# Masked attention with four engines in balance: ten double-mask steps at new places, and a transposition queued behind its own step's mask

## The chip, the core and the metric

The kernel runs on one core of a Trainium2 chip. The core has five engines that follow queues of their own and wait for each other by semaphores: TensorE (PE, matrix products; its weight loads are shown apart as PEld), VectorE (DVE), ScalarE (ACT), GpSimd (POOL), and SyncE (SP), which here only issues DMAs. The metric is the device time of one execution in microseconds (us); lower is better.

## What is computed

Three graph attention layers with eight heads of 16, each followed by a feed-forward part, and then a last layer of a different kind, on 16 sequences of 1024 tokens with 128 features. One adjacency matrix of 1024 x 1024 serves all sequences. Cut to what matters here:

```python
Q, K, V = ((h @ W).reshape(B, N, 8, 16) for W in (Wq, Wk, Wv))
scores = einsum('bnhd,bmhd->bhnm', Q, K) / sqrt(16)
scores = where(adj == 0, -inf, scores)
x = h + (einsum('bhnm,bmhd->bnhd', softmax(scores), V).reshape(B, N, 128) @ Wo + bo)
x = layer_norm(x)
x = layer_norm(x + relu(x @ W1 + b1) @ W2 + b2)      # three times; then
e = leaky_relu(s_i[:, :, None] + s_j[:, None, :])    # last layer, one head
out = layer_norm(softmax(where(adj == 0, -inf, e)) @ (x @ W) + x)
```

## The kernel before

**Tiling.** A block is one sequence in one of the three layers: 48 blocks, numbered 0 to 47, in groups of four sequences (all four in layer 0, then in layer 1, then in layer 2). A block has 32 steps. A step is a choice of head half `g` (four heads), query half `qh` (512 queries) and key tile `kt` (128 keys); eight steps with the same `g` and `qh` make a half, which adds up in one PSUM accumulator, `acc`. Below, "step 11" is the twelfth step of a block.

**One step** (`score_step`, L532). The four heads are two pairs. For each pair TensorE writes the scores of 128 keys by 2 x 512 queries into a PSUM tile `s` (L540); there are three such tiles, and the pool gives a new pair one that is free. The scores become masked exponentials in the SBUF tile `e` in one of two ways:

- by POOL: ScalarE takes the exponential out of PSUM (L548), and POOL multiplies it by a 0/1 mask in SBUF (L549). Only the first pair of a step can go this way.
- by VectorE: VectorE adds a large negative mask while it reads PSUM (L552), and ScalarE takes the exponential in SBUF (L564). The second pair always goes this way; the first goes this way too in the steps of a block that the table `BOTH_ON_DVE` (L41) lists.

Four steps later (`AHEAD`, L40) TensorE multiplies the exponentials by the values into `acc` (`av_step`, L566, matmul L569). So the last value matmul of a half comes in step 11, 19, 27 or, of the last half, in step 3 of the next block. After it `finish` (L572) transposes `acc` on VectorE (L580) into `tt`, takes the reciprocal of the row sums (L583), and POOL multiplies them into `A` (L584). There is one `acc`, so the value matmuls of the next half wait for this transposition.

**Other work.** Between the steps the kernel weaves in tasks, by tables of steps (`AT`, L34): the projections of the next block, in which ScalarE takes the upper part `hi` of a projection (L467, L471) and VectorE the remainder `lo` (L468, L472) at steps 9, 11, 17 and 19; the output projection and the two feed-forward matmuls of the block before (L378), with VectorE's transposes of `A` (L598, two of them in step 9, followed by two small range reductions, L448), additions and statistics (L415, L408, L410) and POOL's normalisation (L428 to L436, four or eight slices) and scaling (L627, L506, L510); transposes of `x` by VectorE (L352) and DMA; and, in twelve blocks at the turn of the groups, the tasks of the last layer (`last_tasks`), with masks of their own on VectorE (L776).

**What sets the order.** The order of TensorE, ScalarE and SyncE is the order of the program text (`tc.manual_schedule`). On VectorE and POOL a scheduler chooses by priorities: `soon()` raises the priority of what stands under it, and `tc.issue_after(x)` makes an instruction stand behind `x` in its queue. Two dictionaries hold such anchors: `low[n]` is the remainder taken in step `n`, and `behind["dve"]` is VectorE's latest mask, which in `finish` is the last mask of the step just issued, since `score_step` of a step is called before its `av_step`. A mask in L551 stands behind the remainder of two steps before, where there was one. `finish` in L579 follows the same rule for the transposition: that of step 11 stands behind the remainder of step 9, that of step 19 behind that of step 17, and the other two are free. [...]

Of the kernel before, what the change touches and what calls it, by code (L numbers as in the profile page):

```python
# [37 lines left out]
STACK_AT = 24  # L38
AT_END = {3: (12, 21, 22, 24, 25, 26, 27, 28, 30, 31), 2: (8, 9, 13, 14, 15, 16, 17, 18, 20, 21)}
AHEAD = 4  # L40
BOTH_ON_DVE = (2, 6, 7, 8, 17, 21, 23, 25, 26, 29, 30)  # L41
TILES = {"w": 8, "x": LANES + 1, "last": 2}
BLOCKED = -57344.0

# [75 lines left out]
def fast_path(ctx: ExitStack, tc: tile.TileContext, a: dict, out: bass.AP, flag):  # L120
# [24 lines left out]
    head, tail = [True], [False]  # L145
# [182 lines left out]
    def soon():  # L328

        return nullcontext() if head[0] else tc.high_priority(offset=SOON)  # L330
# [185 lines left out]
    behind, low = {}, {}  # L516
# [15 lines left out]
    def score_step(step):  # L532
# [3 lines left out]
        for pp in range(2):  # L536
# [6 lines left out]
            psv = ps.rearrange("p (r q) -> p r q", q=512)  # L543
            both = now[0] % (4 * NT) in BOTH_ON_DVE
            on_pool = pp == 0 and not both
# [26 lines left out]
    def finish(g, qh, acc):  # L572

        def run():
            if g == 0 and qh == 0:
                state["A"] = work.tile([P, 2, 16, G, HD], F32, tag="A", name="A", bufs=1)
                state["recs"] = work.tile([P, G, 2, 16], F32, tag="recs", name="recs", bufs=2)
            tt = work.tile([P, 16, SLOT], F32, tag="tt", name="tt", bufs=1)
            with soon(), tc.issue_after(low[now[0] - 2]) if now[0] - 2 in low else nullcontext():  # L579
                nc.vector.transpose(tt.rearrange("p a b -> p (a b)"), acc)  # L580
            rec = state["recs"][:, g, qh, :]
            with soon():
                nc.vector.reciprocal(rec, tt[:, :, HD])  # L583
                nc.gpsimd.tensor_mul(state["A"][:, qh, :, g, :], tt[:, :, :HD],  # L584
                                     rec[:, :, None].to_broadcast([P, 16, HD]))
        return run
# [243 lines left out]
    now = [0]  # L830
# [404 lines left out]
```

## Time and profile before

| what | before |
|---|---|
| time, median of 3 runs | 3988.66 us (3985.82 to 3991.97) |
| time of the profiled execution | 3988.0 us |
| its span, first to last instruction | 3985.9 us |
| mean granted TensorE clock | 0.975 |

The numbers of the profile are from that one execution. "Busy" is the time in which an engine executes something; instructions that follow each other overlap a little, so that a mean duration is longer than the distance between two starts. In the table of groups each row is a line of the kernel on one engine: what it writes and reads with the sizes, how often, then total busy time in us and mean in ns, then the idle time of the engine just ahead of these instructions and who ended it. Two more of its rows belong to the change:

```profile
L569 PE MATMUL acc<-e,v 128*17 128x512 f32 x12288 | 1641.5, 606 | 52.2 <-POOL e L549 48.1
L580 DVE STREAM_TRANSPOSE tt<-acc 128x512 f32<-128x512 f32 x192 | 135.6, 706 | 36.2 <-PE acc L569 36.2
```

The first is the value matmul, the second the transposition of a finished half: its 36.2 us of idle time are spent waiting for the last value matmul of that half.

### The profile page before, as it was taken

What the parts mean: (1) busy time and instruction counts of PE and PEld (TensorE: products, weight loads), DVE (VectorE), ACT (ScalarE), POOL (GpSimd) and SP (SyncE); (2) the same over time, 40 slices, a digit from 0 to 9 for tenths busy, and PEclk for the clock granted to TensorE, in tenths of its full rate; (3) what the DMA queues carried; (4) which work ended last, traced back from release to release, by engine and by line L of the source; (5) the groups of instructions that cost most, each with busy time, mean ns of one, the idle gap of its engine ahead of it and who ended that gap; (6) DMA issues with size and microseconds to landing.
All of it is one profiled execution on the core that took longest, in us unless ns stands there. A gap on an engine that the chain in (4) does not pass through costs nothing.

```text
span 3985.9 us, 108397 instructions
## 1 busy us (share of the span) xinstructions
PE 3735.5 (94%) x43873; PEld 1501.6 (38%) x43873; DVE 3480.8 (87%) x5844; ACT 3289.4 (83%) x3797; POOL 3393.9 (85%) x2923
## 2 busy tenths in 40 slices
PE   7999999999999999998999999999999999999887
PEld 2333333344433333334444333333444433333346
DVE  6889999988889999998888999998888899999765
ACT  7989999977778999996776999998767799999750
POOL 4889999977789999997778999998778899999784
PEclk8999999999999999999999999999999999999998
DMA  5423424322223424332222423333222333324100
GB/s 139 114 65 92 100 71 111 80 66 65 66 66 87 111 69 104 84 90 67 62 67 68 112 67 102 88 85 98 66 55 66 86 75 99 94 73 115 49 7 20
DMA packets 245880, 319.19 MB, mean 80 GB/s; under 512 B 51072, under 2 KB 174208, under 8 KB 245376
## 3 DMA queue, kind: packets, MB, share of 16 engines
q1 hardware_dynamic: 243840, 311.52, 31.3%
q8 instruction: 349, 5.72, 0.6%
q14 instruction: 155, 1.27, 0.1%
q10 hardware_dynamic: 1536, 0.68, 0.1%
HBM read 58.53 MB, written 51.38 MB: 28 GB/s over the span
## 4 chain that ended last, share of the span: by engine, by line
PE 44%; DVE 23%; ACT 10%; POOL 8%; issue 6%; SPq 2%; DMA 1%; ACTq 0%; DVEq 0%; POOLq 0%
PE acc L569 16%; DVE e L552 16%; PE t L378 14%; PE s L540 11%; ACT e L564 5%; ACT e L548 3%; POOL e L549 2%; ACT hT L644 2%; POOL x L436 2%; PE s L378 1%; POOL x L440 1%; DVE st L408 1%; POOL x L441 1%; POOL mv L430 1%; DVE aT L598 1%
## 5 line engine op out<-in xcount | busy, mean ns | idle before, releaser
L552 DVE TENSOR_TENSOR e<-s,mask_add 128x1024 f32<-128x1024 f32 x2064 | 2410.6, 1209 | 166.7 <-PE s L540 133.6
L549 POOL TENSOR_TENSOR e<-e,mask 128x1024 f32<-128x1024 f32 x1008 | 2030.6, 2029 | 436.3 <-ACT e L548 435.5
L564 ACT ACTIVATE e<-e 128x1024 f32<-128x1024 f32 x2064 | 2145.0, 1061 | 190.6 <-DVE e L552 171.6
L569 PE MATMUL acc<-e,v 128*17 128x512 f32 x12288 | 1641.5, 606 | 52.2 <-POOL e L549 48.1
L540 PE MATMUL s<-Wq,Wk 64*128 64x512 f32 x6144 | 1237.7, 464 | 84.6 <-ACT e L548 29.8
L548 ACT ACTIVATE e<-s 128x1024 f32<-128x1024 f32 x1008 | 1032.2, 1024 | 311.7 <-PE s L540 311.0
L540 PEld LDWEIGHTS s<-Wq,Wk 64*128 64x128 f32 x6144 | 509.0, 186 | 1218.4 <-DVE e L552 492.6
L569 PEld LDWEIGHTS acc<-e,v 128*17 128x17 f32 x12288 | 205.6, 95 | 552.3 <-issue 418.4
L436 POOL TENSOR_SCALAR x<-x,mv 128x128 f32<-128x128 f32 x896 | 391.3, 453 | 19.2
L430 POOL TENSOR_TENSOR mv<-mv,half_neg 128x4 f32<-128x4 f32 (+1 forms) x179 | 214.3, 1197 | 14.7
L415 DVE TENSOR_TENSOR x<-t,x 128x512 f32<-128x512 f32 x191 | 132.0, 691 | 106.0 <-PE t L378 102.4
L378 PE MATMUL t<-x1T,W 128*32 128x512 f32 x1520 | 200.8, 600 | 5.1 <-DVE parts L743 3.2
L408 DVE BATCH_NORM_STATS2 st<-x 128x6 f32<-128x128 f32 x896 | 198.1, 281 | 6.3
L378 PEld LDWEIGHTS t<-W,hT 128*32 128x32 f32 x6080 | 173.8, 112 | 63.9 <-issue 57.0
L378 PE MATMUL t<-hd,e 128*32 128x129 f32 x6656 | 194.9, 274 | 3.0 <-DVE lo L468 3.0
L776 DVE SCALAR_TENSOR_TENSOR e<-s,mask 128x256 f32<-128x256 f32 x512 | 175.1, 411 | 22.0 <-PE s L772 21.9
L378 PE MATMUL t<-W,hT 128*32 128x128 f32 x6080 | 187.7, 276 | 2.9 <-DVE parts L743 2.9
L378 PEld LDWEIGHTS t<-hd,e 128*32 128x32 f32 x6656 | 182.1, 109 | 17.3 <-DVE lo L468 6.3
L580 DVE STREAM_TRANSPOSE tt<-acc 128x512 f32<-128x512 f32 x192 | 135.6, 706 | 36.2 <-PE acc L569 36.2
L644 ACT ACTIVATE hT<-t,b 128x512 f32<-128x512 f32 x190 | 131.0, 690 | 22.5 <-PE t L378 21.8
L510 POOL TENSOR_TENSOR x<-x,bo 128x1024 f32<-128x1024 f32 x48 | 114.9, 2393 | 9.7 <-PE s L378 7.2
L584 POOL TENSOR_TENSOR A<-tt,recs 128x256 f32<-128x256 f32 x192 | 120.3, 627 | 3.0 <-DVE recs L583 3.0
(141 smaller groups left out, 2450.1 us busy)
## 6 DMA issues: line engine op xcount, KB each, us to landing
Wk<-hi SPq DMA_DIRECT2D x384, 128.0 KB
Wk<-lo SPq DMA_DIRECT2D x384, 128.0 KB
Wq<-hi SPq DMA_DIRECT2D x384, 128.0 KB
Wq<-lo SPq DMA_DIRECT2D x384, 128.0 KB
tr<-xb SPq DMA_DIRECT2D x656, 64.0 KB
x1T<-tr SPq DMA_DIRECT2D x90, 256.0 KB
xT<-tr SPq DMA_DIRECT2D x74, 256.0 KB
x<-in_x_dram SPq DMA_DIRECT2D x124, 64.0 KB
```

The costliest lines, as they stand in the source:

```text
L378: nc.tensor.matmul(dst[j:j + SLOT, :], cols, rhs, start=start, stop=stop)
L408: nc.vector.bn_stats(st[:, t, :], z[:, t, :])
L430: nc.gpsimd.tensor_tensor(v, v, half_neg[:, ts], OP.pow)
L436: nc.gpsimd.tensor_scalar(z[:, t, :], z[:, t, :], mv[:, t, 0:1], mv[:, t, 1:2], op0=OP.add, op1=OP.mult)
L540: nc.tensor.matmul(ps[:, r * 512:(r + 1) * 512], k[64 * r:64 * r + 64, kt * P:(kt + 1) * P], q[64 * r:64 * r + 64, q0:q0 + 512], start=Tru ...
L548: nc.scalar.activation(ev, psv, AF.Exp, scale=HD ** -0.5)
L549: behind["pool"] = nc.gpsimd.tensor_mul(ev, ev, m).ins
L552: behind["dve"] = nc.vector.tensor_add(ev, psv, m).ins
L564: nc.scalar.activation(ev, ev, AF.Exp, scale=HD ** -0.5)
L569: nc.tensor.matmul(acc[j * SLOT:j * SLOT + HD + 1, :], v_bufs[m % 2][:, kt, 2 * j + g, :], e[:, j, :], start=first, stop=last)
L644: nc.scalar.activation(s["h", f, h], ps, AF.Relu, bias=w["b1"][:, f:f + 1], scale=1.0)
L776: nc.vector.scalar_tensor_tensor(e[:, c + 2 * i, :], ps[:, i * 256:(i + 1) * 256], 1.0, queries(mask01[:, c + 2 * i, half]), op0=OP.max, o ...
```

## The change

Two edits. The table of steps in which VectorE masks both pairs has ten entries in place of eleven, and of the new ten only 7, 8, 23, 26 and 30 were in the old one. In the other steps the first pair goes by ScalarE and POOL. And the transposition in `finish` is issued behind VectorE's latest mask in every half, in place of behind the remainder of two steps before where there is one. `tail[0]` is false wherever `finish` is called.

```diff
-BOTH_ON_DVE = (2, 6, 7, 8, 17, 21, 23, 25, 26, 29, 30)
+BOTH_ON_DVE = (3, 7, 8, 15, 23, 24, 26, 28, 30, 31)
@@ finish
             tt = work.tile([P, 16, SLOT], F32, tag="tt", name="tt", bufs=1)
-            with soon(), tc.issue_after(low[now[0] - 2]) if now[0] - 2 in low else nullcontext():
+            with soon(), tc.issue_after(behind["dve"]) if not tail[0] else nullcontext():
                 nc.vector.transpose(tt.rearrange("p a b -> p (a b)"), acc)
```

## The prediction

> **What bounds the kernel now.** I read the engine totals first, then the share in 40 slices, then the stretches block by block, and in one plain block the timelines of TensorE and POOL. The totals say that four engines are close together, and that none can be given work for nothing:
>
> ```profile
> PE 3735.5 (94%) x43873; PEld 1501.6 (38%) x43873; DVE 3480.8 (87%) x5844; ACT 3289.4 (83%) x3797; POOL 3393.9 (85%) x2923
> L552 DVE TENSOR_TENSOR e<-s,mask_add 128x1024 f32<-128x1024 f32 x2064 | 2410.6, 1209 | 166.7 <-PE s L540 133.6
> L549 POOL TENSOR_TENSOR e<-e,mask 128x1024 f32<-128x1024 f32 x1008 | 2030.6, 2029 | 436.3 <-ACT e L548 435.5
> L564 ACT ACTIVATE e<-e 128x1024 f32<-128x1024 f32 x2064 | 2145.0, 1061 | 190.6 <-DVE e L552 171.6
> ```
>
> The stretches (columns: window; us; busy us and count of PE, PEld, DVE, ACT, POOL; granted clock; DMA) show two kinds of block. 28 of the 48 are alike and take 70.9 us each; twelve that carry the last layer's tasks take 95 to 105.
>
> ```profile
> 1590.16:1661.03 70.87, 69.11 (x710) 24.24 (x706) 66.45 (x99) 66.88 (x74) 65.90 (x55) 1.00 0.37 90
> 939.86:1042.84 102.98, 94.28 (x1333) 45.64 (x1329) 83.01 (x164) 71.17 (x89) 79.86 (x74) 0.95 0.25 64
> 1042.84:1140.18 97.34, 91.61 (x1334) 43.53 (x1331) 83.03 (x164) 71.09 (x89) 80.77 (x74) 0.98 0.26 67
> ```
>
> In a plain block TensorE has the least idle time, 1.76 us. The timeline (start, length, engine and line; idle time before and what ended it in brackets) says where it waits: the second pair of a step finds no free score buffer until VectorE or ScalarE has read an older pair.
>
> ```profile
> 1614.26 0.49 PE L540 MATMUL s<-Wq,Wk 64*128 64x512 f32 x2 [0.41 <-DVE e L552]
> 1615.81 0.72 DVE L580 STREAM_TRANSPOSE tt<-acc 128x512 f32<-128x512 f32 x1 [0.94 <-PE acc L569]
> 1618.93 0.50 PE L540 MATMUL s<-Wq,Wk 64*128 64x512 f32 x2 [0.26 <-DVE e L552]
> 1632.28 0.50 PE L540 MATMUL s<-Wq,Wk 64*128 64x512 f32 x2 [0.60 <-ACT e L548]
> 1654.11 1.05 PE L569 MATMUL acc<-e,v 128*17 128x512 f32 x8
> ```
>
> The same steps are longer than an unhindered one by more than the idle time: a second pair normally starts 0.34 us after the first, and step by step the excess is 0.22 (step 3), 0.25 (9), 0.56 (11), 0.42 (13), 0.76 (19), 0.32 (23), 0.14 (25), 0.34 (29) and 0.2 in small ones: 3.2 us a block that TensorE could win. POOL runs beside it with few gaps:
>
> ```profile
> 1600.53 4.02 POOL L549 TENSOR_TENSOR e<-e,mask 128x1024 f32<-128x1024 f32 x2 [0.22 <-ACT e L548]
> 1611.59 2.03 POOL L549 TENSOR_TENSOR e<-e,mask 128x1024 f32<-128x1024 f32 x1 [1.04 <-ACT e L548]
> 1614.02 4.01 POOL L549 TENSOR_TENSOR e<-e,mask 128x1024 f32<-128x1024 f32 x2 [0.40 <-ACT e L548]
> 1622.92 2.03 POOL L549 TENSOR_TENSOR e<-e,mask 128x1024 f32<-128x1024 f32 x1 [0.35 <-ACT e L548]
> 1646.97 2.02 POOL L549 TENSOR_TENSOR e<-e,mask 128x1024 f32<-128x1024 f32 x1
> ```
>
> From 1622.92 to the end of the block it never waits again, and its products for steps 18, 19, 20 end 0.69, 0.78 and 0.72 us before the value matmuls of those steps (four steps later) start. So POOL is a hair behind TensorE as the limit.
>
> [...] 69.11 of 70.87 us is "busy", yet 3.2 us are stretched waits. [...]
>
> **The change part by part.**
>
> Masks. Per block VectorE masks 42 pairs instead of 43 and POOL 22 instead of 21. Back to back a VectorE mask takes 1.14 us (its starts in the timeline), a POOL product 1.98 (half of 4.01). 48 blocks: VectorE -55 us, POOL +95. ScalarE's count of exponentials stays 64; only their order changes. Steps 2, 6, 17, 21, 25, 29 go to POOL; 3, 15, 24, 28, 31 leave it. No DMA is moved; the scatter of x waits for VectorE's transposes of x, which stay in their steps.
>
> What TensorE wins in a plain block, by working VectorE's queue forward from step 6. With one mask less at step 6, VectorE no longer runs late into steps 7 to 9: step 9's 0.25 goes. Step 11's pair waits for step 10's mask, which still stands behind two transposes of `A` (1.29 us) and two range reductions: 0.46 of 0.56 stays. Steps 17, 21 and 25 with POOL empty VectorE before steps 19, 23, 25: 0.76, 0.32 and 0.14 go, and the built program of the changed kernel no longer takes the freshest score buffer at step 25. Of 29 and 3 about 0.1 stays each.
>
> Transposition. In the built program before, 33 of the 48 transpositions at step 11 stand ahead of their own step's mask (two elsewhere); after, none of the 192. In the lines above VectorE stands idle 0.94 us for the value matmuls with the mask of step 11 queued behind it; that mask starts at 1616.45, and could start at 1614.9, when its scores (from 1614.26) are there. Then step 13 waits 0.26 of its 0.42. The transposition now waits behind the mask, with the reciprocal, the remainder `lo` and step 12's mask queued behind it; it would end at 1616.8 (mask from 1614.9, 1.14, then 0.72) against 1616.5 now, still ahead of the next half's first value matmul at 1617.19, which needs the accumulator free. I take its cost as 0, between 0 and 0.2. Sum for TensorE: about 1.0 of 3.2 left, a gain of 2.2 a block if nothing else bound it.
>
> What POOL allows. From the first product after its long gap (step 4, 1600.53, tied to ScalarE and so to TensorE) its new queue up to step 25's product is: 17 products (steps 4, 5, 6, 9 to 14, 16 to 22 and 25: 16 x 1.985 + 2.03 = 33.8), one normalisation of eight (5.92), two of four (6.96), two A products (1.16), two L627 (4.70), some 0.5 of issue gaps: 53.0 us. Before, the value matmul of step 25 starts at 1654.11, 53.58 after the same point. POOL therefore lets it come 0.4 to 0.5 us earlier, not 2.2: the gaps of 1.04, 0.40 and 0.35 us absorb 1.8 of the extra product at step 6, the swap 15 for 17 is neutral, 21 and 25 come in the place of 24 and 28 but earlier. With 0.1 at step 3, which lies outside that stretch, a plain block wins 0.5 us (between 0.1 and 0.9, since it is the difference of two long sums): 28 x 0.5 = 14 us.
>
> The twelve long blocks. There POOL already stops TensorE; for instance:
>
> ```profile
> 1010.13 2.04 POOL L549 TENSOR_TENSOR e<-e,mask 128x1024 f32<-128x1024 f32 x1
> 1012.22 1.05 PE L569 MATMUL acc<-e,v 128*17 128x512 f32 x8 [0.62 <-POOL e L549]
> 1124.97 1.05 PE L569 MATMUL acc<-e,v 128*17 128x512 f32 x8 [1.79 <-POOL e L549]
> ```
>
> The first (steps 18 and 19, with 4.35 us behind it) has the same number of products ahead before and after. The second, step 22 of the block from 1042.84, gets step 21's product ahead of it: +2.0, against about 1.0 won at its step 6, three times: +3. In the blocks before and behind it VectorE's masks stop TensorE at step 8 for 0.43 and for 1.45 us, of which a mask less wins some 0.6 each: -4. Start, end and the four blocks of 75 us: -3. Together -4, unsure by 10 either way.
>
> Sum: -14 - 4 = -18 us on the profiled execution's 3988.0 (span 3985.9), which lies 0.7 under the median of 3988.66: 3970.
>
> **Rivals.**
> (1) Slower: POOL becomes the limit of every plain block. Place: step 6's product, ahead of the eight-fold normalisation. If its 1.98 us isn't absorbed by the three gaps, steps 18 to 20 are late by 1.98 less the 0.7 of slack, 1.3 us a block: 28 x 1.3 + 3 x 2 in the long blocks = +42, 4031; half absorbed, 4008. It decides as soon as less than 1.3 us of the gaps is left. For it: POOL's 93% in the plain block, rising to 67.9 of 70.9. Against: all three gaps end with a ScalarE exponential whose time hardly moves.
> (2) Faster: POOL is not in the way, and TensorE gets its 2.2: 28 x 2.2 + 8 = 70, 3919. Against it stands the sum of 53.0.
> (3) No change: the 14 us of the plain blocks are given back in the long ones, where stalls of POOL grow by 1 us a block more than I take: 3987. For it: VectorE and POOL there follow tasks that the table of steps does not know.
>
> **How the numbers follow.** About 0.2%, 8 us, is what a measurement of this kernel can tell from no change. Chances: my sum 0.55, own range 3956 to 3984; (1) 0.20; (2) 0.10; (3) 0.15. The range 3938 to 4008 leaves out half of each outer rival. Faster: 0.52 of my case, 0.10 and 0.03: 0.65. Same: 0.03 and 0.10: 0.13. Slower: 0.20 and 0.02: 0.22.
>
> **What would show it.** Plain blocks at about 70.4 us; TensorE's waits for VectorE's masks down, but a wait of the value matmuls for POOL's product new at steps 18 to 25, 0.3 to 2 us a block; POOL at 67.9 us a block; VectorE's wait for the accumulator (36.2 us over the run) nearly gone; the score wait at step 11 still there, that at step 19 gone. Wrong if plain blocks take over 70.9 (rival 1), or if they fall under 69.5 without value matmuls waiting for POOL (rival 2).

## The result, and the profile after

| what | before | after |
|---|---|---|
| time, median of 5 runs each | 3986.06 us (3984.99 to 3991.97) | 3969.53 us (3960.29 to 3972.04) |
| time of the profiled execution | 3988.0 us | 3960.3 us |
| its span | 3985.9 us | 3958.5 us |

The ratio of the means is 0.9951, with a 95% interval of 0.9936 to 0.9965: 0.5% or 20 us faster by the means, 16 us by the medians. The forecast was 3970.0. One caution goes with everything read from the trace of after: its execution was the fastest of its five, 9 us below their median, so the 27 us between the two spans are not the gain. Blocks of one kind can be compared; sums over the whole span only roughly.

The engine totals and the groups of the changed kernel:

```profile
PE 3706.3 (94%) x43873; PEld 1494.8 (38%) x43873; DVE 3424.9 (87%) x5796; ACT 3295.3 (83%) x3797; POOL 3485.5 (88%) x2971
L552 DVE TENSOR_TENSOR e<-s,mask_add 128x1024 f32<-128x1024 f32 x2016 | 2369.3, 1211 | 266.0 <-PE s L540 206.6
L549 POOL TENSOR_TENSOR e<-e,mask 128x1024 f32<-128x1024 f32 x1056 | 2121.1, 2032 | 276.3 <-ACT e L548 275.5
L569 PE MATMUL acc<-e,v 128*17 128x512 f32 x12288 | 1641.6, 606 | 119.8 <-POOL e L549 111.7
L540 PE MATMUL s<-Wq,Wk 64*128 64x512 f32 x6144 | 1204.8, 460 | 42.5 <-DVE e L552 21.2
L580 DVE STREAM_TRANSPOSE tt<-acc 128x512 f32<-128x512 f32 x192 | 135.2, 704 | 3.1 <-PE acc L569 3.1
```

48 masks went from VectorE to POOL, as the table says. The row to look at is the value matmul, L569: TensorE's idle time ahead of it rose from 52.2 to 119.8 us, nearly all for POOL's products, while VectorE's wait for TensorE's scores (L552) rose from 133.6 to 206.6. VectorE was early where it had been late, and POOL the other way round. The transposition's 36.2 us of waiting fell to 3.1.

The chain of work that ended last says the same in one line. First the kernel before, then the changed one (shares of the span by engine):

```profile
PE 44%; DVE 23%; ACT 10%; POOL 8%; issue 6%; SPq 2%; DMA 1%; ACTq 0%; DVEq 0%; POOLq 0%
```

```profile
POOL 50%; PE 33%; DVE 6%; ACT 5%; issue 3%; SPq 1%; DMA 1%; ACTq 0%; DVEq 0%; POOLq 0%
```

A plain block (block 20) and a long one (block 13) of the changed kernel, in the view of stretches with the columns given in the prediction:

```profile
1577.82:1648.27 70.45, 68.56 (x709) 24.09 (x705) 65.37 (x99) 67.10 (x75) 67.75 (x56) 1.00 0.37 92
1031.28:1130.45 99.17, 91.23 (x1333) 43.88 (x1329) 82.09 (x164) 71.49 (x90) 81.89 (x74) 0.97 0.25 66
```

The plain block went from 70.87 to 70.45 us. TensorE's timeline in it, at steps 11, 22, 23, 25 and 29:

```profile
1601.48 0.50 PE L540 MATMUL s<-Wq,Wk 64*128 64x512 f32 x2 [0.42 <-DVE e L552]
...
1626.05 1.05 PE L569 MATMUL acc<-e,v 128*17 128x512 f32 x8 [0.57 <-POOL e L549]
1627.03 0.73 PE L540 MATMUL s<-Wq,Wk 64*128 64x512 f32 x4
1628.03 1.05 PE L569 MATMUL acc<-e,v 128*17 128x512 f32 x8 [0.26 <-POOL e L549]
...
1632.58 0.62 PE L569 MATMUL acc<-e,v 128*17 128x512 f32 x4 [0.28 <-POOL e L549]
...
1641.38 1.05 PE L569 MATMUL acc<-e,v 128*17 128x512 f32 x8 [0.30 <-POOL e L549]
```

Before, every wait in such a block was one for a free score buffer, ahead of L540. Of these only step 11's is left (0.06 at step 17 is new); those of steps 3, 9, 13, 19, 23 and 29 are gone. In their place stand four waits of the value matmuls for POOL's products of steps 18, 19, 21 and 25, 1.41 us together. So idle time alone doesn't show the gain: TensorE idles 1.89 us after and 1.76 before. What fell is its "busy" time, from 69.11 to 68.56, in which the stretched steps were counted.

By kind of block, in the two profiled executions (sums in us):

| blocks | before | after | difference |
|---|---|---|---|
| 28 plain | 1983.6 | 1972.7 | -10.9 |
| 10, 22, 34 | 226.2 | 229.8 | +3.6 |
| 11, 23, 35 | 315.9 | 303.9 | -12.0 |
| 12, 24, 36 | 306.5 | 301.2 | -5.3 |
| 13, 25, 37 | 291.5 | 297.5 | +6.0 |
| 14, 26, 38 | 288.2 | 285.9 | -2.3 |

Blocks 10, 22, 34 and the ones behind them belong together: at the start of block 11 TensorE waits for a DMA (`h_rows<-parts`, 3.19 us before, none after), and a later end of block 10 shortens that wait; the two rows make -8.4. Only the first row is firm: in the trace of the table alone (below), a kernel just as fast, the plain blocks come to -10.8 too, but the fifteen others of this table to +1.9 in place of -10.0: the sums of the long blocks differ by some 10 us between two executions.

### The profile page after: what moved, and what is told of

It reads as the page before. It is cut to its first block, busy times and chain, and to the rows that moved or that the text cites. A ratio compares the mean times of both kernels' runs of the same rounds, so it can differ in the third digit from the quotient of the medians.

```text
span 3958.5 us, 108389 instructions
## 1 busy us (share of the span) xinstructions
PE 3706.3 (94%) x43873; PEld 1494.8 (38%) x43873; DVE 3424.9 (87%) x5796; ACT 3295.3 (83%) x3797; POOL 3485.5 (88%) x2971
## 4 chain that ended last, share of the span: by engine, by line
POOL 50%; PE 33%; DVE 6%; ACT 5%; issue 3%; SPq 1%; DMA 1%; ACTq 0%; DVEq 0%; POOLq 0%
POOL e L549 28%; PE acc L569 12%; PE t L378 10%; PE s L540 8%; POOL x L436 8%; POOL mv L430 4%; POOL x L627 3%; DVE e L552 3%; ACT e L548 3%; ACT e L564 2%; POOL x L440 2%; POOL x L441 2%; PE s L378 2%; POOL A L584 1%; POOL mv L429 1%
## 5 line engine op out<-in xcount | busy, mean ns | idle before, releaser
L552 DVE TENSOR_TENSOR e<-s,mask_add 128x1024 f32<-128x1024 f32 x2016 | 2369.3, 1211 | 266.0 <-PE s L540 206.6
L549 POOL TENSOR_TENSOR e<-e,mask 128x1024 f32<-128x1024 f32 x1056 | 2121.1, 2032 | 276.3 <-ACT e L548 275.5
L564 ACT ACTIVATE e<-e 128x1024 f32<-128x1024 f32 x2016 | 2111.0, 1062 | 120.5 <-DVE e L552 101.2
L569 PE MATMUL acc<-e,v 128*17 128x512 f32 x12288 | 1641.6, 606 | 119.8 <-POOL e L549 111.7
L548 ACT ACTIVATE e<-s 128x1024 f32<-128x1024 f32 x1056 | 1084.4, 1027 | 320.2 <-PE s L540 316.8
L540 PE MATMUL s<-Wq,Wk 64*128 64x512 f32 x6144 | 1204.8, 460 | 42.5 <-DVE e L552 21.2
L540 PEld LDWEIGHTS s<-Wq,Wk 64*128 64x128 f32 x6144 | 504.4, 186 | 1139.6 <-issue 403.8
L569 PEld LDWEIGHTS acc<-e,v 128*17 128x17 f32 x12288 | 204.8, 95 | 637.5 <-issue 360.0
```

What stands on the lines that cost most here:

```text
L540: nc.tensor.matmul(ps[:, r * 512:(r + 1) * 512], k[64 * r:64 * r + 64, kt * P:(kt + 1) * P], q[64 * r:64 * r + 64, q0:q0 + 512], start=Tru ...
L548: nc.scalar.activation(ev, psv, AF.Exp, scale=HD ** -0.5)
L549: behind["pool"] = nc.gpsimd.tensor_mul(ev, ev, m).ins
L552: behind["dve"] = nc.vector.tensor_add(ev, psv, m).ins
L564: nc.scalar.activation(ev, ev, AF.Exp, scale=HD ** -0.5)
L569: nc.tensor.matmul(acc[j * SLOT:j * SLOT + HD + 1, :], v_bufs[m % 2][:, kt, 2 * j + g, :], e[:, j, :], start=first, stop=last)
```

## The experiments

All ratios are against runs of the kernel before on the same chip.

### The two edits apart

The first kernel has the new table alone, the second the new rule for the transposition alone.

```diff
-BOTH_ON_DVE = (2, 6, 7, 8, 17, 21, 23, 25, 26, 29, 30)
+BOTH_ON_DVE = (3, 7, 8, 15, 23, 24, 26, 28, 30, 31)
```

> Only the table of the change, with the old rule for the transposition. Theory (the table carries the gain, the transposition costs and brings next to nothing): 3966 to 3976 us, plain blocks 70.4 to 70.7 us, value matmuls waiting for POOL's products at steps 22 to 29 as with the whole change, and VectorE's wait for the accumulator still some 20 to 36 us over the run. Rival (the gain comes from the transposition that no longer holds up a mask): 3982 us or more, plain blocks 70.8 or more.

> Only the new rule for the transposition, with the old table of eleven steps. Theory: 3976 to 3986 us; of TensorE's wait at step 13 of a plain block (0.42 us) 0.26 may go, 7 us over 28 blocks, the rest of the waits for score buffers (steps 3, 9, 19, 23, 29) stays as before; VectorE's wait for the accumulator nearly gone. Rival (the transposition carries the gain): 3966 to 3974 us. Second rival (the transposition behind the mask makes the next half's value matmuls late): 3988 or more, with new waits of the value matmuls for VectorE.

Measured: the table alone 3966.53 us, ratio 0.9951 [0.9938, 0.9965], the same as both edits; the transposition alone 3980.88 us, 0.9989 [0.9980, 0.9997], a small gain. VectorE's wait for the accumulator stays at 35.1 us over the run with the first and falls to 3.5 with the second. The stretch of block 20, first with the table alone, then with the transposition alone:

```profile
1575.60:1646.04 70.44, 68.62 (x709) 24.10 (x706) 65.13 (x99) 67.05 (x75) 67.77 (x56) 1.00 0.36 92
```

```profile
1582.96:1653.50 70.54, 69.05 (x709) 24.23 (x706) 66.72 (x99) 66.86 (x74) 65.79 (x55) 1.00 0.34 88
```

Each edit alone takes 0.43 or 0.33 us from a plain block, and the two together 0.42, not 0.76. TensorE's timeline with the table alone (steps 13, 22, 23 and 25) says why:

```profile
1603.91 0.51 PE L540 MATMUL s<-Wq,Wk 64*128 64x512 f32 x2 [0.25 <-DVE e L552]
...
1623.81 1.05 PE L569 MATMUL acc<-e,v 128*17 128x512 f32 x8 [0.27 <-POOL e L549]
...
1625.79 1.05 PE L569 MATMUL acc<-e,v 128*17 128x512 f32 x8 [0.27 <-POOL e L549]
...
1630.35 1.05 PE L569 MATMUL acc<-e,v 128*17 128x512 f32 x8 [0.27 <-POOL e L549]
```

Step 13 still waits 0.25 us for the mask that the transposition holds up, and step 22 waits 0.27 for POOL. With both edits the first wait is gone and the second is 0.57: what TensorE wins at step 13 it stands idle at step 22, because POOL's product comes at its own time. With the old table POOL is not late, and there the same 0.25 us are kept.

### Is POOL the limit, and which part of its queue

Two attempts to shorten POOL's queue without moving work to another engine. The first leaves out the addition of the feed-forward bias in L627 (2.4 us on POOL), in the changed kernel and in the kernel before:

```diff
-                    op(s["n1"][0], s["n1"][0], rows(w[v]))
+                    if v != "b2": op(s["n1"][0], s["n1"][0], rows(w[v]))
```

> The changed kernel without POOL's addition of the second feed-forward bias in L627 (left out of the computation: 2.35 us of POOL's queue in each block that has it); nothing else moves. Theory (POOL's queue from step 4 to step 25 is the limit of a plain block after the change): the waits of the value matmuls at steps 22, 23, 25 and 29 (1.41 us in one block) go, plain blocks 69.0 to 69.5 us, and with the long blocks some 50 us in all: 3910 to 3930. Rival (these waits only take the place of others, and TensorE with VectorE sets the pace): plain blocks 70.2 or more, 3955 to 3965, by the long blocks alone.

> The kernel before without the same addition. Theory (there the free score buffers stop TensorE, and POOL has 0.7 us of slack): plain blocks 70.7 to 70.9 us, no gain there; the blocks in which POOL stopped TensorE win about 2 us each, some 15 us in all: 3968 to 3978. Rival (POOL sets the pace before as well): plain blocks 69.8 or less, 3945 or less.

Measured: changed kernel 3950.77 us, 0.9912 [0.9899, 0.9926]; kernel before 3983.81 us, 0.9995 [0.9987, 1.0004]. The first is a miss for both theories: block 20 takes 70.08 us, a gain of 0.37 of the 2.4, where 69.0 to 69.5 or at least 70.2 were expected. TensorE's timeline in it shows which waits went:

```profile
1620.02 1.05 PE L569 MATMUL acc<-e,v 128*17 128x512 f32 x8 [0.57 <-POOL e L549]
...
1622.00 1.05 PE L569 MATMUL acc<-e,v 128*17 128x512 f32 x8 [0.26 <-POOL e L549]
...
1626.55 1.05 PE L569 MATMUL acc<-e,v 128*17 128x512 f32 x8 [0.27 <-POOL e L549]
...
1634.98 1.05 PE L569 MATMUL acc<-e,v 128*17 128x512 f32 x8
```

Only the last one, at step 29. The reason is in POOL's timeline of the changed kernel:

```profile
1623.97 4.00 POOL L549 TENSOR_TENSOR e<-e,mask 128x1024 f32<-128x1024 f32 x2
1627.93 0.62 POOL L584 TENSOR_TENSOR A<-tt,recs 128x256 f32<-128x256 f32 x1
1628.51 6.00 POOL L549 TENSOR_TENSOR e<-e,mask 128x1024 f32<-128x1024 f32 x3
1634.44 2.42 POOL L627 TENSOR_TENSOR x<-x,ln_g 128x1024 f32<-128x1024 f32 x1
```

The products of steps 18 to 22 are the two and the three; the scaling and the bias of L627 stand behind them. What was taken out could not shorten the queue ahead of the waits at steps 22, 23 and 25. (In the kernel before, a plain block takes 70.80 us, as its theory had it. The gain of 15 us expected in its long blocks didn't come: in block 13 of that kernel both L627 stand behind the product that TensorE waits for.)

The second attempt takes the time away ahead of step 18's product: POOL's products of steps 10 and 12 cover half of the queries.

```diff
-                behind["pool"] = nc.gpsimd.tensor_mul(ev, ev, m).ins
+                n = 256 if now[0] % (4 * NT) in (10, 12) else 512
+                behind["pool"] = nc.gpsimd.tensor_mul(ev[:, :, :n], ev[:, :, :n], m[:, :, :n]).ins
```

> The changed kernel with POOL's products of steps 10 and 12 over half of the queries only (the other half of these two pairs stays unmasked): some 1.9 us less in POOL's queue ahead of step 18's product, and nothing moved to another engine. Theory (POOL's queue from step 4's product to step 21's is the limit of a plain block): the waits of the value matmuls at steps 22, 23, 25 and 29 (1.41 us in one block) go, plain blocks 69.0 to 69.5 us, 3928 to 3945. Rival (something else holds the pace): plain blocks 70.2 or more, 3960 or more.

> The kernel before with the same two half products. Theory (before the change the score buffers stop TensorE, POOL has 0.7 us of slack): plain blocks 70.7 to 70.9 us, no more than 0.2 us less than before; 3975 to 3986. Rival (POOL sets the pace before as well): plain blocks 69.8 or less, 3955 or less.

Measured: changed kernel 3929.65 us, 0.9858 [0.9843, 0.9873]; kernel before 3976.87 us, 0.9978 [0.9968, 0.9988]. Block 20, first of the changed kernel with the half products, then of the kernel before with them:

```profile
1567.06:1636.54 69.48, 68.60 (x709) 24.22 (x706) 65.39 (x99) 66.63 (x75) 65.93 (x56) 1.00 0.37 96
```

```profile
1582.32:1653.22 70.90, 69.16 (x708) 24.24 (x705) 66.47 (x99) 66.89 (x74) 64.06 (x55) 1.00 0.34 87
```

POOL has 1.8 us less to do in both. After the change a plain block wins 0.97 us of it; before the change it wins nothing. That shows the shift of the limit: the same relief, in the same place, counts only once the new table has made POOL the last to arrive. (The 9 us that the kernel before wins lie outside the plain blocks; in the profiled execution 5.2 of them in blocks 11, 23 and 35 and 3.3 in the first three blocks.) The waits at steps 22 and 23 are gone in TensorE's timeline; what is left is step 11's 0.41, 0.13 at step 25 and step 29's 0.28.

### Giving a step back to VectorE

```diff
-BOTH_ON_DVE = (3, 7, 8, 15, 23, 24, 26, 28, 30, 31)
+BOTH_ON_DVE = (3, 6, 7, 8, 15, 23, 24, 26, 28, 30, 31)
```

> The changed kernel with step 6 back in the table (eleven entries): POOL has one product less, 1.98 us, ahead of step 18's. Theory (POOL's queue up to the products of steps 18 to 21 is what limits a plain block now, and VectorE has room again): the waits of the value matmuls at steps 22, 23 and 25 (1.11 us in one block) go, VectorE's lateness at step 9 (0.25) returns, plain blocks 69.4 to 69.9 us; 3940 to 3955. Rival (VectorE is the limit as soon as it masks step 6 as well): plain blocks 70.4 or more, 3966 or more.

Measured: 3953.82 us, 0.9921 [0.9907, 0.9934], and 0.68 us less in a plain block:

```profile
1572.91:1642.68 69.77, 68.83 (x708) 24.27 (x705) 66.34 (x100) 66.72 (x75) 65.78 (x55) 1.00 0.36 95
```

TensorE's waits at steps 22 and 23 are gone, 0.11 and 0.27 us stay at steps 25 and 29, and VectorE's at step 9 is back with 0.09. So the gain of the change doesn't come from having ten steps instead of eleven: with eleven, step 6 among them, the kernel wins 0.8% instead of 0.5%. VectorE had room for one more mask in a plain block, and POOL had none.

### The long blocks

In blocks 13, 25 and 37 TensorE waits 5.16 us at step 26 (1.79 before). TensorE's timeline of the changed kernel around that wait, and the stretches of the wait, of what follows and of what follows that:

```profile
1107.96 0.74 PE L540 MATMUL s<-Wq,Wk 64*128 64x512 f32 x4
1113.86 1.91 PE L569 MATMUL acc<-e,v 128*17 128x512 f32 x8 [5.16 <-POOL e L549]
1115.54 1.52 PE L378 MATMUL t<-w_nodes,xT 128*32 128x130 f32 x24
1116.99 0.94 PE L540 MATMUL s<-Wq,Wk 64*128 64x512 f32 x4
1117.87 1.05 PE L569 MATMUL acc<-e,v 128*17 128x512 f32 x8
```

```profile
1108.69:1113.85 5.16, 0.00 (x1) 0.00 (x0) 2.24 (x2) 2.17 (x3) 5.00 (x6) 0.69 0.77 198
1113.85:1117.30 3.45, 3.44 (x34) 1.62 (x36) 0.00 (x0) 0.17 (x2) 3.37 (x2) 0.50 0.63 168
1117.30:1120.50 3.20, 3.20 (x28) 1.01 (x30) 2.91 (x6) 2.95 (x8) 3.20 (x2) 0.97 0.08 21
```

Eight value matmuls take 1.91 us right behind the wait and 1.05 a step later: the granted clock is 0.50 over these 3.45 us. The long wait is paid twice: from the start of this matmul to the end of the block TensorE takes 16.60 us where it took 15.20 before. In blocks 10, 22 and 34 the same follows waits of 2.80, 2.80 and 2.79 us at step 21 (0.83, 0.82 and 0.83 us for four value matmuls, 0.44 at full pace). An experiment takes products out of POOL's queue in these six blocks alone:

```diff
+MORE = {10: (17,), 22: (17,), 34: (17,), 13: (21, 22), 25: (21, 22), 37: (21, 22)}
...
-            both = now[0] % (4 * NT) in BOTH_ON_DVE
+            both = now[0] % (4 * NT) in BOTH_ON_DVE + MORE.get(now[0] // (4 * NT), ())
```

> The changed kernel with more masks on VectorE in six long blocks only: step 17 in blocks 10, 22, 34, steps 21 and 22 in blocks 13, 25, 37. Behind TensorE's long waits there (2.80 and 5.16 us) its matmuls start 0.83 us apart for four instead of 0.44. Theory (the wait costs a second time through the half speed behind it, about 1.4 us): blocks 10, 22, 34 win more than the 1.98 us of the product taken away, 2.5 to 3.5 us each, with no half speed left; blocks 13, 25, 37 win 4 to 6 us each; 3942 to 3955. Rival (VectorE, with its own tasks of the last layer there, takes over as the limit): less than 1 us a block, 3965 or more.

Measured: 3949.55 us, 0.9910 [0.9895, 0.9925]. Blocks 13, 25, 37 take 286.0 us where they took 297.5, 3.8 each, a little less than expected; a wait of 1.34 us at step 23 for one of VectorE's last-layer tasks is part of it (none for VectorE there in the changed kernel). TensorE's timeline of block 13 at step 26 has no wait and no half speed left (from L42 on, the lines of this kernel are numbered one higher):

```profile
1113.96 1.05 PE L570 MATMUL acc<-e,v 128*17 128x512 f32 x8
1114.83 0.85 PE L379 MATMUL t<-w_nodes,xT 128*32 128x130 f32 x24
```

Blocks 10, 22, 34 take 218.8 us where they took 229.8, 3.7 each for one product of 1.98. But this doesn't stay: at the start of blocks 11, 23, 35 TensorE comes earlier to the transfer and waits for it, 4.23, 4.13 and 4.83 us where it waited 0, 1.25 and 0.98 (the last for `g_rows`). In block 11:

```profile
831.85 1.19 PE L773 MATMUL s<-g_rows,h_rows 4*128 4x256 f32 x7 [4.23 <-DMA h_rows<-parts]
```

These three blocks take 318.9 us where they took 303.9, so that the two kinds together take 537.7 in place of 533.7. Of the six blocks only 13, 25 and 37 show a gain that lasts in these two executions.

### A kernel that beats both

Step 6 and the six blocks together, and then step 19 on VectorE too in blocks 11, 12, 23, 24, 35 and 36:

```diff
-MORE = {10: (17,), 22: (17,), 34: (17,), 13: (21, 22), 25: (21, 22), 37: (21, 22)}
+MORE = {10: (17,), 22: (17,), 34: (17,), 13: (21, 22), 25: (21, 22), 37: (21, 22), 11: (19,), 12: (19,), 23: (19,), 24: (19,), 35: (19,), 36: (19,)}
```

> Step 6 back in the table, and the six long blocks with their extra masks on VectorE (step 17 in blocks 10, 22, 34; steps 21 and 22 in 13, 25, 37). Theory (two separate places of POOL's queue, each a limit where it stands): the gains add up but for blocks 10, 22, 34, whose wait step 6 has already shortened to 1.7 us: 3930 to 3942 us, plain blocks 69.7 to 69.9. Rival (one gain takes the place of the other): 3947 or more.

> As the one before it, and step 19 on VectorE in blocks 11, 12, 23, 24, 35, 36, where the value matmul of step 19 waits 4.34 us for POOL and half speed often follows. Theory (the product stands behind two long POOL instructions of 4.7 us; taken away, the next wait is step 20's, some 1.5 us): 3 to 5 us a block, 3906 to 3925 us. Rival (VectorE, with the last layer's tasks at these steps, comes late with the extra mask): less than 1 us a block, within 5 us of the one before.

Measured: 3939.21 us, 0.9882 [0.9867, 0.9897], and 3921.06 us, 0.9831 [0.9818, 0.9845]: 1.7% faster than the kernel before. Both times lie where their theories had them. The gains of step 6 (plain blocks of 69.8 us) and of blocks 13, 25, 37 (284.8 us for the three) add up; blocks 10, 22, 34 with the ones behind them take 539.4 us, no less than with step 6 alone (538.4), for the same transfer. In the last kernel blocks 11, 12 and their like win 3.6 us each over the one before it (309.2 + 293.7 against 320.7 + 303.6 us, six blocks), and behind a wait no value matmul but those of the last block starts slowly (mean granted clock 0.978, against 0.974 in the changed kernel). The longest wait that is left in block 11 is the one for the transfer:

```profile
830.40 1.01 PE L773 MATMUL s<-g_rows,h_rows 4*128 4x256 f32 x7 [4.54 <-DMA h_rows<-parts]
```

## Why the prediction was right, and where it was not

**Plain blocks: -0.5 forecast, -0.45 measured** in the 25 that follow another plain block; the three behind a long one gained nothing (70.36 before, 70.47 after), so the 28 gave -10.9 where -14 was forecast. The mechanism is the forecast one: TensorE's waits for score buffers fall, and POOL's queue caps what that brings. The half products show it, since they count after and not before.

**The sum that fixed the cap named too long a queue.** The prediction took POOL's queue "up to step 25's product", 53.0 us; it took 53.3 in the trace, and the value matmul of step 25 comes 0.28 us earlier by that count, not 0.4 to 0.5. But the first product that comes too late is step 18's, and nothing behind it can be the cause, as the left-out bias addition showed. The right sum is shorter: from the start of step 4's product to the end of step 18's POOL took 37.60 us before and 37.91 after, 0.31 more, so that 1.67 of the extra product's 1.98 us were absorbed (1.8 forecast). The slack at step 18 was 0.69. The difference, 0.38, is what TensorE could come earlier, and with 0.1 at step 3 that is 0.48, close to the 0.5 which the longer sum gave. It was the right number from a neighbouring place, in part by luck.

**The waits one by one.** Step 11's wait stays (0.42), as forecast, and those of steps 9, 19, 23 and 25 are gone. Steps 3 and 13 have no idle time left either, where a small rest was forecast to stay at both. POOL's 67.75 us a block and VectorE's wait for the accumulator, 3.1 us, are as forecast. Which move of the table ends which wait was argued from VectorE's queue; of the moves, only that of step 6 was taken back by itself.

**Transposition.** Its cost of 0 in the changed kernel is right, and shown by the table alone being as fast as both. As an edit of its own it is worth 0.33 us a plain block, because with the old table POOL has the slack (0.69 us at step 18).

**Rivals.** (1), POOL as a limit slower than the old one, fell because 1.67 of the 1.98 us were absorbed. (2), TensorE winning 2.2 us a block, fell too: the four waits for POOL are there, and with POOL's load lightened a plain block still takes 69.5 to 69.8, not 68.7 (some 0.4 us of it are still waits for POOL). (3), a gain given back in the long blocks, happened in two kinds of block out of five and not in the sum. Two of the rivals' times don't follow from their own terms: with half of the product absorbed, 0.99 less 0.7 of slack is 0.3 us a block, about 4003 and not 4008; and 1 us more in each of twelve long blocks gives 3982, not 3987. Neither decided anything.

**Long blocks: the terms behind the -4 failed.** For blocks 13, 25, 37 the forecast was +2.0 for step 21's product less 1.0 won earlier, +3 in all; it was +6.0. What the trace of block 13 shows is a product of step 22 that ends only 0.45 us later in the block, with TensorE 2.9 us earlier in front of it, and 1.40 us lost behind the wait at half speed. For blocks 10, 22, 34, which the forecast counted in with "-3", it was +3.6, by a wait of 2.80 us for step 17's product and the half speed behind it. Blocks 11, 23, 35 gave more than that back, partly because their wait for the transfer shrank. Of the 1.45 us that TensorE waits at step 8 of block 14, some 0.6 were to go; the wait stayed (1.46). These fifteen blocks came to -10.0 in the profiled executions, everything else but the plain blocks to -6.5 more: past the -4 with its 10 either way, though in an execution that lies 9 us under its median. By the medians, all but the plain blocks won some 6 us (16.5 less 10.9), by the means 9: near the forecast, but by luck, since its terms were off in both directions.

## What to carry to other kernels

Here four engines were within a few per cent of each other (65.9 to 69.1 us busy of the 70.87 of a plain block), and two edits that won 0.43 and 0.33 us apart won 0.42 together: each moved the moment of arrival of one engine, and only the last to arrive counted. So ask of each wait which instruction it ends with, and of the engine that ends it only what stands ahead of that instruction in its queue; a block's totals, or a queue summed too far, can give a good number for a wrong reason. A table that serves all blocks is worth splitting where some blocks carry other work: two masks that the plain blocks leave to POOL won 3.8 us a block on VectorE in blocks 13, 25 and 37. And look at what stands behind the block that wins: what blocks 10, 22 and 34 won, 3.7 us each, was spent waiting for a transfer (4.23 us in block 11).

## What the runs showed of the hardware

In these traces TensorE's longer waits had a price behind them. Over all twelve traces, of the waits of value matmuls outside the last block, all 62 between 1.2 and 2.4 us were followed by matmuls at full pace (0.44 us for four); of 18 between 2.4 and 2.7 us, five were followed by half pace (0.83); of 15 between 2.7 and 3.5 us, 13; of 60 between 3.5 and 4.5 us, 46, and six fell between; above 4.5 us all 15. In block 13 shown above half pace lasted 3.6 us behind the wait, and the block lost some 1.4 us by it. In each of the twelve traces all changes of the granted clock, between 1.0 and 0.5, lie on one grid of 3.413 us, to within 0.01 us, and which waits were followed by half pace went by how they fell on that grid. Here are two waits of 2.62 us in the kernel with the table alone, in stretches of that grid, in blocks 23 and 35:

```profile
1862.46:1865.87 3.41, 1.26 (x12) 0.30 (x4) 2.75 (x3) 3.25 (x4) 3.33 (x3) 1.00 0.15 38
1865.87:1869.28 3.41, 2.94 (x32) 1.32 (x32) 0.00 (x0) 0.00 (x0) 3.33 (x3) 0.50 0.44 126
```

```profile
2831.84:2835.26 3.42, 2.04 (x16) 0.43 (x12) 3.31 (x4) 3.42 (x7) 3.34 (x3) 1.00 0.03 8
2835.26:2838.67 3.41, 2.17 (x36) 1.13 (x36) 0.22 (x2) 0.99 (x5) 3.41 (x2) 1.00 0.31 80
2838.67:2842.08 3.41, 0.20 (x2) 0.00 (x0) 2.77 (x4) 2.12 (x4) 3.33 (x3) 1.00 0.84 239
```

The first has 2.15 us in one stretch, TensorE is busy for 1.26 of it, and the next stretch has half the clock. The second is cut into 1.38 and 1.24 us, and the clock stays. The 18 waits between 2.4 and 2.7 us part in the same way: the five followed by half pace have 2.06 to 2.49 us in one stretch, the other 13 at most 1.97. And of the waits between 3.5 and 4.5 us, the eight with full pace behind them have their larger part in a stretch that ends after the wait, where the clock falls 0.4 to 1.0 us later. So about 2 us of waiting within one stretch were enough here; why the clock falls, the traces don't show. The prediction had this cost in no term, though the waits of 4.35 us in blocks 11 and 12 of the kernel before already carried it: four value matmuls took 0.83 us behind both.
